# A routed two-layer graph network: pair loads that wait for their own chunk's sends, and an allotment issued in pieces

## The chip, the cores and the metric

The kernel runs on one core of a Trainium2 chip. The core has a tensor engine (PE, with its weight loads shown apart as PEld), a vector engine (DVE), a scalar engine (ACT), GpSimd (POOL), and SyncE (SP), which here only issues transfers; 16 DMA engines move data between HBM and the on-chip memory for all of them. Each engine works off its own list of instructions in order and waits on semaphores for the others. The metric is the device time of one execution in microseconds (us), the median of several runs.

## The reference

The input `x` is 64 batches of 256 rows of 256 numbers (float32); `adj` is one 256 x 256 adjacency shared by all batches. Two layers run one after the other:

```
x = x + gnn0(layernorm(x))        # 4 heads, softmax over neighbours, elu
x = x + layernorm(x) @ Wf.T + bf
x = x + gnn1(layernorm(x))        # 1 head, relu
x = x + moe(layernorm(x))         # 8 experts, the two best of each row

def moe(tokens):
    probs = softmax(tokens @ router_w.T)
    rw, re = top_k(probs, 2);  rw = rw / rw.sum(-1)
    out = tokens
    for e in range(8):
        y = gelu(tokens @ w1[e] + b1[e]) @ w2[e] + b2[e]
        out = out + combine[:, e] * y      # combine: rw at re, else 0
```

The last step matters here: each row is sent to two of eight experts.

## The kernel before

**Work and tiles.** Each batch is two tiles of 128 rows. `batch_layers` computes the first three lines of the reference and the normalised rows `xng` for one batch; PE does the transposes and products, DVE and ACT the attention and the norms, and POOL the inverse roots (`rstd`, lines 407, 408, 445, 448). Near the end (`at_end`) DVE computes these roots itself.

**Routing.** Of the 64 batches 61 are routed, in 20 chunks: twelve of four batches, then five of two and three of one. The last three batches are dense: every expert is computed for every row and weighted. For a chunk, `route` finds the two best experts of each row (`top_two`), counts rows of each expert with two small products (`pp`), and gets each row's place in a region of its expert in a buffer `xs` in HBM. `send` (line 1054) then writes 128 rows of 260 numbers with one indirect DMA issued by POOL (line 1056), two for each tile: 244 sends in all. A step of the program sends one tile, so a chunk of four batches is sent over eight steps.

**Pairs.** Every 256 rows of one expert make a pair, and a full pair can be computed. `allot` (line 826) works out which pairs a chunk completed. It is 19 small DVE instructions in a generator of four parts: lines 833 to 839, 842 to 851, 854 to 862, 864 to 870. It gives `ids` (the expert and the place of each pair), which SP reads into registers (lines 881, 885), and `ef`. For a chunk of four batches (`spread`) the parts are issued at four of its tiles; for a smaller chunk all four are issued at once by `in_one`, ahead of the sends.

`expert_pair` computes one pair: SP loads its rows from `xs` (`xr`, four DMAs, line 892, and `xt`, line 903) and the expert's first weights (`we`, line 917); DVE turns the rows (`sT`); PE makes `ph` (line 950), ACT the Gelu (`hT`, line 956), PE `py` (line 965), DVE adds the bias (`y`, line 975), ACT scales the rows (line 943). Then `scatter` adds the 256 rows to the output with two indirect DMAs of POOL (line 986). Each scatter waits for the two adds before it (line 983), and for the plain stores (`out_dram<-base`, line 735) that precede it. There are 129 pairs: 115 full ones and 14 of the flush, which holds what is left in each expert's region. Before the flush is loaded, SP writes `fill` behind the last row of each of the eight regions (line 1168), at places that it reads from `ends_at` (line 1162).

**Waits.** A framework derives waits from what instructions read and write. `xs` is one tensor addressed through registers, so it takes any two accesses for a conflict unless told otherwise. Sends and fills are told not to wait for each other or for loads (group "rows"). A pair load is not told so: it waits for every send and fill issued before it in the program, besides those in `needs`, its own chunk's.

**Order.** The program is written under a manual schedule. All work consists of generators with a rank; in each step the active ones are advanced by rank, lowest first, and `yield r` gives the rank in the next step (a negative number: later in the same step). A batch begins every three steps. Until step 177 (`DRAIN_AT`) up to two pairs begin in every three steps, afterwards one in each step, and one scatter is issued per step for each pair that is ready. The order of the instructions on each engine is fixed by this when the kernel is built. Buffers: `xr` 5, `we` 7, `sT` 3, `hT` 5, `y` 9, `xt` 14.

Of the kernel before, what the change touches and what calls it, by code (L numbers as in the profile page):

```python
# [17 lines left out]
SYNC = mybir.DependencyQuery.ANY_SYNC  # L18
AFTER = mybir.DependencyInfo(mybir.DependencyClass.Sync, mybir.DependencyReason.DATA)
# [8 lines left out]
def kernel(  # L28
# [23 lines left out]
    NT = N // P  # L52
# [23 lines left out]
    keep = ctx.enter_context(tc.tile_pool(name="keep", bufs=1))  # L76
# [416 lines left out]
    for i in range(2):  # L493
        t = keep.tile([P, NT, D + 1], F32, tag=f"q1_{i}", name=f"q1_{i}")
# [280 lines left out]
    def in_one(parts):  # L775

        got = None
        for got in parts:
            pass
        return got  # L780
# [38 lines left out]
    rows = [keep.tile([P, E], F32, tag="rows", name="rows")]  # L819
# [56 lines left out]
    def expert_pair(j, n, ids, ef, regs, needs):  # L876

        i = j % GROUP
        upto = min(j + GROUP, n)
        if i == 0:  # L880
            _, regs["e"] = nc.values_load_multi_w_load_instructions(
                ids[0:1, 0, j:upto], engines=[mybir.EngineType.SP], min_val=0, max_val=E - 1,
                skip_runtime_bounds_check_because=WHY,
            )
            _, regs["t"] = nc.values_load_multi_w_load_instructions(
                ids[0:1, 1, j:upto], engines=[mybir.EngineType.SP], min_val=0, max_val=E * CAP,
                skip_runtime_bounds_check_because=WHY,
            )
        e_sp, t_sp = regs["e"][i], regs["t"][i]
        xr = io.tile([P, PAIR // S, KT * S], F32, tag="xr", name="xr", bufs=XBUFS)  # L890
        loads = [
            nc.sync.dma_start(  # L892
                out=xr[g * S : (g + 1) * S],
                in_=xs_d.rearrange("(t c q) f -> t q c f", c=PAIR // S, q=S)[
                    bass.ds(t_sp, 1), :, :, g * KT * S : (g + 1) * KT * S
                ].rearrange("t q c f -> (t q) c f"),
            )
            for g in range(P // S)
        ]

        xt = small.tile([P, 2, ROW - D], F32, tag="xt", name="xt", bufs=14)
        loads.append(
            nc.sync.dma_start(
                out=xt,
                in_=xs_d.rearrange("(t k p) c -> t p k c", p=P, k=2)[
                    bass.ds(t_sp, 1), :, :, D:
                ].rearrange("t p k c -> (t p) k c"),
            )
        )
        for load in loads:  # L910
            tc.add_to_no_dep_group("rows", load.ins)
            for name in needs:
                tc.add_manual_dep(
                    load.ins, name, AFTER, reason="any sent row may lie in the pair"
                )
        we = io.tile([P, WROW], F32, tag="we", name="we", bufs=WBUFS)
        nc.sync.dma_start(
            out=we, in_=wpack[bass.ds(e_sp, 1), :, :].rearrange("e p c -> (e p) c")
        )
        yield 90  # L920

        yield 95 if more else 75
        xT = turned(work.tile([P, KT, PAIR], F32, tag="sT", name="sT", bufs=3), xr)
        w = small.tile([P, 2], F32, tag="w", name="w", bufs=12)
        yield 30
        yield 30
        hT = hidden(xT, we)
        yield -65
        nc.vector.scalar_tensor_tensor(
            w[:, :, None], xt[:, :, 1:2], ef[:, j : j + 1], xt[:, :, 2:3],  # L930
            op0=ALU.is_equal, op1=ALU.mult,
        )
        nc.vector.tensor_tensor(w[:, :, None], w[:, :, None], xt[:, :, 3:4], ALU.add)
        yield 80
        if i == 0:
            _, regs["x"] = nc.values_load_multi_w_load_instructions(
                ids[0:1, 0, j:upto], engines=[mybir.EngineType.PE, mybir.EngineType.DVE],
                min_val=0, max_val=E - 1, skip_runtime_bounds_check_because=WHY,
            )
        y = result(hT, bass.ds(regs["x"][i], 1))  # L940
        yield 2
        for t in range(2):
            nc.scalar.activation(y[:, t, :], y[:, t, :], AF.Copy, scale=w[:, t : t + 1])  # L943
        scatters.append((y, xt))
# [103 lines left out]
    sent = []  # L1048
# [5 lines left out]
    def send(xe, at):  # L1054

        d = nc.gpsimd.indirect_dma_start(  # L1056
            out=xs_d[: E * CAP * PAIR, :],
            out_offset=bass.IndirectOffsetOnAxis(ap=at, axis=0), in_=xe, in_offset=None,
        )
        tc.declare_no_dep(  # L1060
            d.ins, query=SYNC, group="rows", reason="sent rows are all different, and none is in a full pair"
        )
        tc.add_to_no_dep_group("rows", d.ins)
        sent.append(d.ins.name)
        nc.gpsimd.nop()

    def later(rank, *phases):
# [5 lines left out]
    def route(c, row0, nt, n, last, xng, lg):  # L1073
# [3 lines left out]
        spread = nt == NTC  # L1077
# [5 lines left out]
        parts = top_two(c, nt, lg, tail[:, :, 0])  # L1083
# [50 lines left out]
        for i, xe in enumerate(xng):  # L1134
            vec.tensor_copy(xe[:, :, D + 1 :], tail[:, i * NT : (i + 1) * NT, :])
        parts = allot(c, n, False)
        if n and not spread:
            ids, ef = in_one(parts)
        if last:
            ends_at = rt([E], "ends_at", 2, I32)  # L1140
            vec.tensor_copy(ends_at, rows[0])
# [2 lines left out]
        for t in range(nt):  # L1144
            for k in range(2):
                send(xng[t // NT][:, t % NT, :], pos[:, k, t : t + 1])
            if n and spread and t in (1, 2, 4, 5):
                ids, ef = next(parts) or (None, None)
            if not last:
                yield 95  # L1150
            elif t % 2:
                yield 95
        needs = sent[mark:]
        if n:
            regs = {}
# [2 lines left out]
            )  # L1158
        if last:
            parts = allot(c + 1, FLUSH, True)  # L1160
            ids2, ef2 = in_one(parts)
            _, ends_sp = nc.values_load_multi_w_load_instructions(
                ends_at[0:1, :], engines=[mybir.EngineType.SP], min_val=0,
                max_val=(E * CAP - 1) * PAIR, skip_runtime_bounds_check_because="rows of a region",
            )
            filled = []
            for e in range(E):
                d = nc.sync.dma_start(  # L1168
                    out=xs_d[bass.ds(ends_sp[e], PAIR), :].rearrange("(p t) c -> p t c", t=2),
                    in_=fill,  # L1170
                )
                tc.declare_no_dep(
                    d.ins, query=SYNC, group="rows", reason="filling rows lie behind an expert's last row"
                )
                tc.add_to_no_dep_group("rows", d.ins)
                filled.append(d.ins.name)
                nc.sync.nop()
            yield 95
            regs2 = {}
            waiting.extend(  # L1180
                lambda j=j: expert_pair(j, FLUSH, ids2, ef2, regs2, filled)
                for j in range(FLUSH)
            )
# [131 lines left out]
```

## Time and profile before

| what | value |
|---|---|
| median of 3 runs | 1519.05 us (1517.03 to 1519.11) |
| the profiled execution | 1516.68 us |
| its span, first to last instruction | 1514.9 us |
| mean granted clock of PE over the span | 0.985 |
| sends (line 1056): number, mean on POOL | 244, 1089 ns |
| scatters (line 986): number, mean on POOL | 258, 1604 ns |
| HBM read and written | 146.00 MB, 88.35 MB |
| SP's longest waits | L622 for DVE 176.7 us, L735 for ACT 123.9 us, L892 for sends 121.1 us |

Times in a timeline count from the span's start. The durations in the profile are of one execution, so sums are made against its own 1516.68 us. A row such as `SPq L892 <- DMA xs<-xng,pos` reads: the queue of SP stood at line 892 until a DMA that writes `xs` from `xng` had landed. Busy time of POOL in a scatter or send is the time of writing its descriptors; the transfer runs on behind it. Where a releaser is named that can't be needed (an `hT` for a scatter), it merely ended at about the same time.

### The profile page before, as it was taken

What the parts mean: (1) busy time and instruction counts of PE and PEld (TensorE: products, weight loads), DVE (VectorE), ACT (ScalarE), POOL (GpSimd) and SP (SyncE); (2) the same over time, 40 slices, a digit from 0 to 9 for tenths busy, and PEclk for the clock granted to TensorE, in tenths of its full rate; (3) what the DMA queues carried; (4) which work ended last, traced back from release to release, by engine and by line L of the source; (5) the groups of instructions that cost most, each with busy time, mean ns of one, the idle gap of its engine ahead of it and who ended that gap; (6) DMA issues with size and microseconds to landing.
All of it is one profiled execution on the core that took longest, in us unless ns stands there. A gap on an engine that the chain in (4) does not pass through costs nothing. (4 is left out here: it accounts for less than half of the span.)

```text
span 1514.9 us, 29999 instructions
## 1 busy us (share of the span) xinstructions
PE 1421.4 (94%) x8134; PEld 1261.2 (83%) x8134; DVE 1245.9 (82%) x4419; ACT 1017.4 (67%) x2396; POOL 875.8 (58%) x845
## 2 busy tenths in 40 slices
PE   7899999999999999999999999998899989699992
PEld 6698888789898989999998989997788877578881
DVE  7689999989898889888898989899888878654541
ACT  1477667677778777777777777776678779553330
POOL 2122546455858586767676676756747776544444
PEclk9999999999999999999999999999999999999996
DMA  4822334576878788787877787867768676797743
GB/s 129 244 91 73 117 103 139 134 178 158 198 154 192 162 194 171 170 183 166 181 181 164 175 185 160 187 156 166 172 154 186 132 162 128 174 208 156 142 65 52
DMA packets 354355, 236.38 MB, mean 156 GB/s; under 512 B 246276, under 2 KB 316428, under 8 KB 354188
## 3 DMA queue, kind: packets, MB, share of 16 engines
q1 hardware_dynamic: 301272, 158.16, 41.7%
q0 software_dynamic: 48864, 66.33, 24.3%
q10 hardware_dynamic: 4052, 9.98, 2.1%
q8 instruction: 67, 1.10, 0.3%
q14 instruction: 100, 0.82, 0.2%
HBM read 146.00 MB, written 88.35 MB: 155 GB/s over the span
## 5 line engine op out<-in xcount | busy, mean ns | idle before, releaser
L986 POOL DMA_INDIRECT out_dram<-y,xt x258 | 413.9, 1604 | 195.7 <-issue 66.6
L585 PE MATMUL pv<-q,z 128*128 128x65 f32 (+1 forms) x2560 | 362.6, 296 | 0.4
L585 PEld LDWEIGHTS pv<-q,z 128*128 128x128 f32 x2560 | 329.9, 193 | 13.0 <-DVE z L571 1.1
L1056 POOL DMA_INDIRECT xs<-xng,pos x244 | 265.7, 1089 | 65.4 <-issue 59.8
L965 PE MATMUL py<-w2s,hT 128*128 (+1 forms) x1224 | 280.6, 380 | 6.3 <-ACT hT L956 6.3
L965 PEld LDWEIGHTS py<-w2s,hT 128*128 128x128 f32 x1224 | 228.3, 190 | 38.3 <-ACT hT L956 9.1
L950 PE MATMUL ph<-sT,we 128*128 128x256 f32 x1032 | 244.2, 387 | 14.9 <-DMA we<-wpack 8.8
L571 DVE SCALAR_TENSOR_TENSOR z<-z,q,mask 128x256 f32<-128x256 f32 x504 | 231.5, 482 | 14.7 <-DMA z<-terms 5.7
L950 PEld LDWEIGHTS ph<-sT,we 128*128 128x128 f32 x1032 | 198.0, 194 | 43.6 <-issue 10.3
L460 ACT COPY xT<-pt 128x512 f32<-128x512 f32 x209 | 121.3, 588 | 99.2 <-PE pt L454 76.6
L943 ACT ACTIVATE y<-y,w 128x256 f32<-128x256 f32 x258 | 112.9, 498 | 110.2 <-DVE y L975 93.6
L956 ACT ACTIVATE hT<-ph,we 128x256 f32<-128x256 f32 x306 | 123.9, 473 | 63.0 <-PE ph L950 42.4
L407 POOL TENSOR_SCALAR rstd<-mv 128x4 f32<-128x4 f32 (+1 forms) x66 | 15.6, 236 | 248.1 <-DVE mv L380 194.7
L425 ACT ACTIVATE off<-x,sums 128x256 f32<-128x256 f32 x256 | 129.4, 505 | 7.9 <-DVE x L668 1.7
L505 PE MATMUL pq<-wx,xT 128*128 128x259 f32 x512 | 125.3, 387 | 9.6 <-ACT xT L460 6.9
L470 PE MATMUL pq<-wx,xT 128*128 128x268 f32 x512 | 128.1, 394 | 1.5 <-ACT xT L460 0.7
L975 DVE TENSOR_TENSOR y<-py,b2s 128x512 f32<-128x512 f32 x129 | 85.9, 685 | 52.4 <-PE py L965 39.4
L661 PE MATMUL pf<-wfT,xT 128*128 128x256 f32 x512 | 122.7, 383 | 0.0
L505 PEld LDWEIGHTS pq<-wx,xT 128*128 128x128 f32 x512 | 94.3, 189 | 30.2 <-ACT xT L460 13.5
L470 PEld LDWEIGHTS pq<-wx,xT 128*128 128x128 f32 x512 | 97.8, 192 | 20.7 <-DVE wx L168 1.3
L689 ACT ACTIVATE rel<-pv,rinv 128x256 f32<-128x256 f32 x128 | 54.4, 470 | 84.5 <-DVE rinv L592 53.8
L661 PEld LDWEIGHTS pf<-wfT,xT 128*128 128x128 f32 x512 | 93.8, 193 | 10.4 <-issue 0.2
(174 smaller groups left out, 2383.7 us busy)
## 6 DMA issues: line engine op xcount, KB each, us to landing
we<-wpack SPq DMA_DIRECT2D x145, 288.0 KB
xr<-xs SPq DMA_DIRECT2D x516, 64.0 KB
z<-terms SPq DMA_DIRECT2D x46, 512.0 KB
xin<-in_x_dram SPq DMA_DIRECT2D x64, 256.0 KB
out_dram<-base SPq DMA_DIRECT2D x61, 256.0 KB
xblk<-in_x_dram SPq DMA_DIRECT2D x188, 64.0 KB
z<-terms ACTq DMA_DIRECT2D x17, 512.0 KB
out_dram<-y,xt POOLq DMA_INDIRECT x258
```

Of the source, the lines that this page charges most:

```text
L425: nc.scalar.activation(off, src[:, t, :], AF.Square, bias=sums[:, t : t + 1], scale=-float(D), accum_out=sq[:, at + t : at + t + 1],)
L460: nc.scalar.copy(dst, pt)
L470: nc.tensor.matmul(pq.rearrange("p h c -> p (h c)"), xT[:, k, t * P : (t + 1) * P], wx[:, k, :], start=(k == 0), stop=(k == KT - 1),)
L505: nc.tensor.matmul(pq, xT[:, k, t * P : (t + 1) * P], wx1[:, k, :], start=(k == 0), stop=(k == KT - 1),)
L571: nc.vector.scalar_tensor_tensor(z[:, j, :, h, :], terms, q[:, j, h, HD + 2 : HD + 3], masks[0][:, j, :].rearrange("p (t i) -> p t i", t=N ...
L585: nc.tensor.matmul(pv[:, h, :], z(j, h, t), q[:, j, h, : d + 1], start=(j == 0), stop=(j == NT - 1),)
L661: nc.tensor.matmul(pf[:, t, :], xT[:, k, t * P : (t + 1) * P], wfT[:, k, :], start=(k == 0), stop=(k == KT - 1),)
L950: nc.tensor.matmul(ph[:, f, :], we[:, k * D + f * P : k * D + (f + 1) * P], xT[:, k, :], start=(k == 0), stop=(k == KT - 1),)
L956: nc.scalar.activation(hT[:, f, :], ph[:, f, :], AF.Gelu, bias=we[:, C_B1 + f : C_B1 + f + 1])
L965: nc.tensor.matmul(py[:, t, :], hT[:, f, t * P : (t + 1) * P], w2s[:, e, f * D : (f + 1) * D].rearrange("p e c -> p (e c)"), start=(f == 0 ...
L986: d = nc.gpsimd.indirect_dma_start(out=out_rows, out_offset=bass.IndirectOffsetOnAxis(ap=xt[:, t, 0:1].bitcast(I32), axis=0), in_=y[:, t, ...
L1056: d = nc.gpsimd.indirect_dma_start(out=xs_d[: E * CAP * PAIR, :], out_offset=bass.IndirectOffsetOnAxis(ap=at, axis=0), in_=xe, in_offset=None,
```

## The change

Three things are edited.

- In `expert_pair`, the five loads of rows are declared independent of all instructions in a new group "sent", which holds every send and every fill, except those in `needs`: the sends of the pair's own chunk, or, for the pairs of the flush, the eight fills. `sent` and `filled` now hold instructions in place of names.
- In `route`, `allot` of a chunk of two batches (four tiles) is issued part by part behind the sends of its tiles 0, 1, 2 and 3; of a chunk of one batch (two tiles) two parts behind tile 0 and two behind tile 1. Chunks of four batches keep theirs at tiles 1, 2, 4 and 5. The chunk that is last now takes a step for each tile like the others, so its four sends are issued in two steps.
- The flush allotment is issued a part at a time ahead of every second fill, and the eight fills over two steps, four in each.

The order in which the instructions stand on the engines follows from the build. PE and ACT keep theirs exactly. On DVE the 19 instructions of each small allotment move from one block ahead of `by` and `stats` (lines 706, 379) to four places, each behind a `y` addition or behind a part of the next routing. On POOL the last chunk's four sends in a row become two, then the two adds of a scatter and an iota, then two. On SP the block of eight fills ahead of the pair loads becomes one pair load, four fills, one pair load, four fills.

```diff
--- before.py
+++ after.py
@@ -908,10 +908,14 @@
             )
         )
         for load in loads:
+            tc.declare_no_dep(
+                load.ins, query=SYNC, group="sent", keep=needs,
+                reason="the pair's rows were sent by these or by sends that earlier loads waited for",
+            )
             tc.add_to_no_dep_group("rows", load.ins)
-            for name in needs:
+            for ins in needs:
                 tc.add_manual_dep(
-                    load.ins, name, AFTER, reason="any sent row may lie in the pair"
+                    load.ins, ins.name, AFTER, reason="any row of these may lie in the pair"
                 )
         we = io.tile([P, WROW], F32, tag="we", name="we", bufs=WBUFS)
         nc.sync.dma_start(
@@ -1061,7 +1065,8 @@
             d.ins, query=SYNC, group="rows", reason="sent rows are all different, and none is in a full pair"
         )
         tc.add_to_no_dep_group("rows", d.ins)
-        sent.append(d.ins.name)
+        tc.add_to_no_dep_group("sent", d.ins)
+        sent.append(d.ins)
         nc.gpsimd.nop()
 
     def later(rank, *phases):
@@ -1134,8 +1139,7 @@
         for i, xe in enumerate(xng):
             vec.tensor_copy(xe[:, :, D + 1 :], tail[:, i * NT : (i + 1) * NT, :])
         parts = allot(c, n, False)
-        if n and not spread:
-            ids, ef = in_one(parts)
+        turns = (1, 2, 4, 5) if spread else (0, 1, 2, 3) if nt == 2 * NT else (0, 0, 1, 1)
         if last:
             ends_at = rt([E], "ends_at", 2, I32)
             vec.tensor_copy(ends_at, rows[0])
@@ -1144,12 +1148,9 @@
         for t in range(nt):
             for k in range(2):
                 send(xng[t // NT][:, t % NT, :], pos[:, k, t : t + 1])
-            if n and spread and t in (1, 2, 4, 5):
+            for _ in range(turns.count(t) if n else 0):
                 ids, ef = next(parts) or (None, None)
-            if not last:
-                yield 95
-            elif t % 2:
-                yield 95
+            yield 95
         needs = sent[mark:]
         if n:
             regs = {}
@@ -1158,13 +1159,14 @@
             )
         if last:
             parts = allot(c + 1, FLUSH, True)
-            ids2, ef2 = in_one(parts)
             _, ends_sp = nc.values_load_multi_w_load_instructions(
                 ends_at[0:1, :], engines=[mybir.EngineType.SP], min_val=0,
                 max_val=(E * CAP - 1) * PAIR, skip_runtime_bounds_check_because="rows of a region",
             )
             filled = []
             for e in range(E):
+                if e % 2 == 0:
+                    ids2, ef2 = next(parts) or (None, None)
                 d = nc.sync.dma_start(
                     out=xs_d[bass.ds(ends_sp[e], PAIR), :].rearrange("(p t) c -> p t c", t=2),
                     in_=fill,
@@ -1173,9 +1175,11 @@
                     d.ins, query=SYNC, group="rows", reason="filling rows lie behind an expert's last row"
                 )
                 tc.add_to_no_dep_group("rows", d.ins)
-                filled.append(d.ins.name)
+                tc.add_to_no_dep_group("sent", d.ins)
+                filled.append(d.ins)
                 nc.sync.nop()
-            yield 95
+                if e % 4 == 3:
+                    yield 95
             regs2 = {}
             waiting.extend(
                 lambda j=j: expert_pair(j, FLUSH, ids2, ef2, regs2, filled)
```

## The prediction

> **What bounds the kernel now.** I read the page first, then windows by stage, the waits of each engine, and last the timelines. The page's engine row says TensorE:
>
> ```profile
> PE 1421.4 (94%) x8134; PEld 1261.2 (83%) x8134; DVE 1245.9 (82%) x4419; ACT 1017.4 (67%) x2396; POOL 875.8 (58%) x845
> ```
>
> The windows split that average (columns: stretch, its us, then PE, PEld, DVE, ACT and POOL busy with counts, PE clock, DMA share, GB/s):
>
> ```profile
> 350.00:1000.00 650.00, 649.57 (x3861) 586.54 (x3860) 583.34 (x2000) 495.90 (x1173) 448.11 (x420) 1.00 0.80 176
> 1000.00:1260.00 260.00, 240.76 (x1348) 211.30 (x1347) 223.04 (x882) 190.84 (x418) 172.49 (x160) 0.98 0.71 158
> 1260.00:1440.00 180.00, 161.39 (x750) 138.41 (x750) 109.75 (x409) 94.75 (x206) 85.95 (x63) 0.98 0.79 165
> 1440.00:1515.00 75.00, 46.97 (x214) 39.99 (x213) 23.38 (x52) 16.00 (x38) 33.95 (x22) 0.85 0.40 58
> ```
>
> Up to 1000 us PE is idle 0.4 us in 650: nothing beside it counts there. From 1000 to 1260 (the chunks of two batches and of one) it is idle 19.2 us. After 1260 another thing rules. The chain of waits shows PE from 1337 to 1470 and the scatters on POOL after it, but the waits of POOL between 1260 and 1515 tell another story: it stands before L986 in nearly every pair, with releasers that change at random.
>
> ```profile
> POOL out_dram L986 <- DMA out_dram<-y,xt: 43.2, 12, 5.2
> POOL out_dram L986 <- ACT hT L956: 29.3, 11, 3.8
> POOL out_dram L986 <- DMA xr<-xs: 23.1, 5, 5.8
> ```
>
> An `hT` or an `xr` releases no scatter; each scatter waits, by L983, for the two adds before it. So I compared two timelines: the scaled `y` of a pair on ACT (L943) and its scatter on POOL, 129 of each in one order. The y of the pair scattered at 1260.43 was ready at 1243.6, that of 1336.75 at 1310.0, of 1434.78 at 1401.5: 17, 27 and 33 us earlier. From 1260 on the scatters are one serial chain that never waits for data: 34 intervals from 1260.43 to 1504.88, 7.19 us each. At the end, with little else on the DMAs, they show their bare form on POOL's timeline:
>
> ```profile
> 1498.58 1.54 POOL L986 DMA_INDIRECT out_dram<-y,xt  x1 [2.95 <-DMA out_dram<-y,xt]
> 1500.43 1.54 POOL L986 DMA_INDIRECT out_dram<-y,xt  x1 [0.30 <-issue]
> 1504.88 1.54 POOL L986 DMA_INDIRECT out_dram<-y,xt  x1 [2.91 <-DMA out_dram<-y,xt]
> ```
>
> So the end is: when POOL can begin this chain, plus 34 intervals. It begins behind the last `rstd` that POOL must wait for, L445 at 1253.13 (idle 4.11, released by ACT `off`), and ACT came to that behind the y of a PE product that ended at 1246.8. Before 1250, therefore, PE's time still counts one for one. Its gaps there, from PE's timeline (start, us, ..., idle before and releaser):
>
> ```profile
> 1043.24 3.72 PE L950 MATMUL ph<-sT,we 128*128 128x256 f32 x16 [2.92 <-DVE sT L117]
> 1051.89 1.36 PE L505 MATMUL pq<-wx,xT 128*128 128x259 f32 x5 [1.91 <-ACT hT L956]
> ...
> 1092.33 1.07 PE L454 MATMUL pt<-ident,x 128*128 128x128 f32 x4 [4.47 <-DVE x L695]
> ```
>
> Others are 1.03 at 1133.30, 1.04 at 1183.05, 1.78 at 1218.35 and 1.67 at 1234.27. Before most of them DVE runs unbroken, with the allotment in front:
>
> ```profile
> 1080.15 0.17 DVE L833 TENSOR_SCALAR full<-run 128x8 f32<-128x8 f32 x1
> ...
> 1083.51 0.17 DVE L870 TENSOR_SCALAR ids<-pair_of 128x4 int32<-128x4 f32 x1
> ...
> 1088.19 1.29 DVE L117 STREAM_TRANSPOSE sT<-xr 128x512 f32<-128x512 f32 x2
> ...
> 1092.19 0.47 DVE L668 SCALAR_TENSOR_TENSOR x<-pf,rstd,x1b 128x256 f32<-128x256 f32 x1
> ```
>
> The 19 small instructions take 3.53 us, and all behind them, `x` of L668 too, comes 3.53 us later.
>
> **What the Trainium skill says.** "TensorE: Matmul & The Clock Gate", the part on array architecture, calls the queues of ACT and DVE strict FIFO: what stands behind the allotment cannot pass it. The trace agrees (no instruction between 1080.15 and 1092.6 starts out of its order). Its Part 1 says that an idle window of about 3.4 us halves PE's clock. The trace agrees: clock 0.50 in 1092.80 to 1096.20, behind the gap of 4.47, and in 1236.20 to 1239.50. "DMA: Bandwidth & Descriptors", Anatomy of one DMA, puts most of a DMA's fixed 2 us into the confirmation of its last byte, and says a semaphore wait is held by the issuing sequencer. Here the wait for a scatter's landing is what spaces the chain, and a pair load that waits on SP holds all of SP's queue.
>
> **The change part by part.** The built order of the changed kernel against the old shows PE and ACT with the same instructions in the same order. DVE, SP and POOL move.
>
> 1. Pair loads no longer wait for later chunks' sends. SP loses most of one row:
>
> ```profile
> SPq L892 <- DMA xs<-xng,pos: 121.1, 24, 9.2
> ```
>
> In chunks of four batches three of the first loads in each group drop one such wait (4 to 6 us each). Behind it on SP stood a `we` load, `terms`, `xin` and `base`. Their users are covered: PE is full until 1000; later `sT` stands 1 to 10 us ahead of its product, and after 1260 the scatters have 17 us in hand. DVE waits for `z<-terms` only 5.7 us in the whole run. Bounds: a gain of 2, a loss of 2 (loads that are earlier meet other transfers); I take 0.
>
> 2. The flush pairs' fills leave the way of ordinary loads. Before, eight fills (5.93 us on SP from 1311.63, the last landing taking 4.57) stood before the load at 1321.58, and PE waited 8.75 us for the pair at 1328.40. In the new order one pair load precedes the fills, another comes between the fours, and no ordinary load waits for a fill. The PE gap mostly goes, but the scatters were 23 us or more behind then: worth 0. Were that cover absent it would be worth 8.75 and 3.4 of a halved clock (6.83 us at half), 12 in all: the upper bound.
>
> 3. Allotment in pieces: 4, 7, 4 and 4 instructions, 0.8, 1.1, 0.8 and 0.9 us from the same rows, one at the end of each of the next steps, chunks of one batch two and two. DVE's sum is the same. Piece one now stands behind `y` (L975), before the `sT` of the next step. Gap by gap: at 1043.24 the lump took 3.78, 0.8 comes back, 2.98 earlier: the 2.92 goes. The 1.91 at 1051.89 hangs on the same late `ph` (one batch earlier it is 0.74): 1.15 goes. At 1092.33, 3.53 less 0.8: 2.7 goes. At 1133.30 and 1183.05 `sT` stood directly behind the lump: 1.0 each. At 1234.27 the lump of 1220.77 to 1224.25 is at the head of an unbroken row: 1.6. The 1.78 at 1218.35 waits for POOL's `rstd`, with no lump before it: stays. Sum 10.35. In return the pieces stand before `x`/`z`, `by` and `sT`, in five chunks: between 0 and 5 x 1.1 = 5.5, I take 2.5, since most `sT` have over 1.1 us in hand but two have 1.55. Net gain 7.9. POOL can follow: its idle waits for `rstd` there (9.97 at 1136.55, 3.85 at 1186.30, 4.11 at 1253.13) stand right behind lumps or PE work and shrink with them. If both halved clocks go as well, 3.4 us x half each, 3.4 more: kept for the range.
>
> 4. The last chunk sends two and two. Its four sends in a row (1300.57 to 1305.46) sit inside the serial chain, in an interval of 8.93 us where the neighbours have about 7.1. Two sends fit behind the adds' landing. The two that move, 2.6 us with their issue, fall into the next interval, which is idle 3.29. Between 1.8 gained and 1 lost; I take a gain of 1.2.
>
> 5. The flush allotment (3.83 us on DVE at 1301.60) split by the fills: behind the scatters' backlog, 0.
>
> Sum: -7.9 - 1.2 = -9.1. Against the profiled execution (span 1514.9, execution 1516.68) this is 1507.6. The median shown, 1519.05, is 2.4 above that; moved by the same 9.1 it gives 1510.
>
> **The rivals.**
> A, the forecast, 1510 (own range 1504 to 1515.5): chance 0.52.
> B, the gaps only move. DVE is busy 223 of 260 us from 1000 to 1260, and the same work stays in the queue; PE could meet `z` or `by` late instead. Only the split sends and a little remain, about 1.5: 1517.5. For it: DVE's density. Against: DVE does wait for PE in between (1.9 us at `lg`, 1.2 at `rinv` from 1050 to 1100), so it has room to catch up. 0.20.
> C, slower: denser DMA stretches the scatters. At a DMA share of 0.40 an interval is 6.35; from 1336.75 to 1434.78, at about 0.79, 7.54: 3 us per unit of share. If loads freed of waits raise the share by 0.1 through 26 intervals, that is 8; with B's 1.5 gained it ends at +6: 1525. It decides once the mean of 34 intervals rises above 7.19 + 9.1/34 = 7.46. Against: bytes are the same, so what crowds early leaves late. 0.15.
> D, the larger gain: halved clocks vanish (3.4) and the loads end sooner against the scatters, whose intervals fall towards 6.35 earlier (five intervals by 1): 1510 - 8.4, about 1502. 0.13.
>
> **How the numbers follow.** About 0.2%, 3 us, is what a measurement of this kernel can tell from no change. Faster (below 1516): A 0.50, D 0.13, B 0.04: 0.67. Within: B 0.15, A 0.02: 0.17. Slower: C and a rest of B: 0.16. The range 1502 to 1521 leaves out most of C and half of D.
>
> **What would show it.** Right: gaps before `ph` at 1043 and `pt` at 1092 under 2 us, the first of the last 35 scatters some 8 us earlier, its distance to the end 1 to 2 us shorter, SP's L892 row for sends a fraction of 121, no 8.75 gap near 1328, and no time saved by that. Wrong: new PE gaps behind `z`, `by` or `sT`; intervals of the last scatters above 7.46; or scatters found waiting for their `y`, so that PE rules to the end.

## The result, and the profile after

| | before | after |
|---|---|---|
| median | 1518.04 us (4 runs, 1516.12 to 1519.11) | 1508.78 us (4 runs, 1505.69 to 1511.43) |
| ratio, with its 95% interval | | 0.9943 (0.9917 to 0.9969) |
| the profiled execution | 1516.68 us | 1511.43 us |
| its span | 1514.9 us | 1509.6 us |
| 34 intervals between the scatters of the last 35 pairs | 244.4 us | 239.3 us |

The change makes the kernel 9.3 us faster by the medians; the profiled execution of the changed kernel is its slowest of four, so that the two traces differ by 5.3 us only. All lines from 912 on stand four or five numbers later (`ph` L950 is L954, the scatter L986 is L990, the send L1056 is L1060, `y` L975 is L979).

The windows of the changed kernel (same columns as before: stretch, its us, then PE, PEld, DVE, ACT and POOL busy, PE clock, DMA share, GB/s):

```profile
350.00:1000.00 650.00, 645.44 (x3817) 581.20 (x3816) 578.77 (x1983) 493.74 (x1163) 444.27 (x417) 1.00 0.76 174
1000.00:1260.00 260.00, 248.53 (x1421) 219.03 (x1419) 231.59 (x906) 199.60 (x445) 174.52 (x165) 0.99 0.74 167
```

From 1000 to 1260 PE is idle 11.5 us in place of 19.2. But from 350 to 1000, where it had been idle 0.4, it is now idle 4.6. The waits of SP's queue, longest first, have lost the row that waited for sends (121.1 us). No row of that kind is left; SP now stands longer further down its list, at L622 (176.7 us before):

```profile
SPq L622 <- DVE stats L379: 327.7, 44, 11.4
SPq L735 <- ACT base L724: 136.6, 15, 11.3
```

PE's timeline at the two largest of the old gaps (2.92 at 1043, 4.47 at 1092):

```profile
1052.55 1.32 PE L954 MATMUL ph<-sT,we 128*128 128x256 f32 x5 [0.79 <-PE pf L661]
...
1099.89 0.84 PE L454 MATMUL pt<-ident,x 128*128 128x128 f32 x4 [0.78 <-issue]
```

And POOL's at the end, where each pair still waits about 3 us for the landing of the adds before it:

```profile
1493.25 1.55 POOL L990 DMA_INDIRECT out_dram<-y,xt  x1 [3.02 <-DMA out_dram<-y,xt]
1495.11 1.55 POOL L990 DMA_INDIRECT out_dram<-y,xt  x1 [0.30 <-issue]
1499.62 1.55 POOL L990 DMA_INDIRECT out_dram<-y,xt  x1 [2.96 <-DMA out_dram<-y,xt]
```

**Where the time went.** PE carries out the same instructions in the same order in both kernels, so its instructions can serve as milestones. I take those that began at 350, 1000 and 1245 us in the trace of before, and for the rest the start of the last 35 scatters and of the last pair's scatter:

| stretch | before | after | difference |
|---|---|---|---|
| start to milestone 350 | 350.1 | 356.5 | +6.4 |
| 350 to 1000 | 650.0 | 655.8 | +5.8 |
| 1000 to 1245 | 245.0 | 233.3 | -11.7 |
| 1245 to the start of the scatter chain | 15.3 | 14.7 | -0.6 |
| the chain, 34 intervals | 244.4 | 239.3 | -5.1 |

The gain is where the prediction put it. Two stretches that the prediction took for unchanged took as much back, before any small chunk was allotted. A milestone difference between two single traces can be the change's or the execution's; the experiments were made to tell which.

### The profile page after: what moved, and what is told of

It reads as the page before. It is cut to its first block, busy times and chain, and to the rows that moved or that the text cites. A ratio compares the mean times of both kernels' runs of the same rounds, so it can differ in the third digit from the quotient of the medians.

```text
span 1509.6 us, 29981 instructions
## 1 busy us (share of the span) xinstructions
PE 1426.9 (95%) x8134; PEld 1264.8 (84%) x8134; DVE 1245.8 (83%) x4419; ACT 1017.4 (67%) x2396; POOL 871.6 (58%) x845
## 5 line engine op out<-in xcount | busy, mean ns | idle before, releaser
L990 POOL DMA_INDIRECT out_dram<-y,xt x258 | 413.1, 1601 | 194.7 <-issue 57.2
L585 PE MATMUL pv<-q,z 128*128 128x65 f32 (+1 forms) x2560 | 366.6, 298 | 0.6
L585 PEld LDWEIGHTS pv<-q,z 128*128 128x128 f32 x2560 | 333.0, 194 | 13.6 <-DVE z L571 1.7
L1060 POOL DMA_INDIRECT xs<-xng,pos x244 | 260.7, 1068 | 65.3 <-issue 59.0
L571 DVE SCALAR_TENSOR_TENSOR z<-z,q,mask 128x256 f32<-128x256 f32 x504 | 231.5, 482 | 17.6 <-DMA z<-terms 8.6
L954 PE MATMUL ph<-sT,we 128*128 128x256 f32 x1032 | 240.0, 382 | 2.5 <-DVE y L979 1.0
L954 PEld LDWEIGHTS ph<-sT,we 128*128 128x128 f32 x1032 | 195.6, 192 | 30.2 <-DVE y L979 1.4
L460 ACT COPY xT<-pt 128x512 f32<-128x512 f32 x209 | 121.6, 590 | 110.7 <-PE pt L454 79.5
L505 PE MATMUL pq<-wx,xT 128*128 128x259 f32 x512 | 128.8, 394 | 15.1 <-ACT xT L460 10.0
L979 DVE TENSOR_TENSOR y<-py,b2s 128x512 f32<-128x512 f32 x129 | 85.4, 684 | 53.9 <-PE py L969 41.8
L505 PEld LDWEIGHTS pq<-wx,xT 128*128 128x128 f32 x512 | 95.6, 192 | 37.9 <-ACT xT L460 17.7
```

The costliest lines, as they stand in the source:

```text
L460: nc.scalar.copy(dst, pt)
L505: nc.tensor.matmul(pq, xT[:, k, t * P : (t + 1) * P], wx1[:, k, :], start=(k == 0), stop=(k == KT - 1),)
L571: nc.vector.scalar_tensor_tensor(z[:, j, :, h, :], terms, q[:, j, h, HD + 2 : HD + 3], masks[0][:, j, :].rearrange("p (t i) -> p t i", t=N ...
L585: nc.tensor.matmul(pv[:, h, :], z(j, h, t), q[:, j, h, : d + 1], start=(j == 0), stop=(j == NT - 1),)
L954: nc.tensor.matmul(ph[:, f, :], we[:, k * D + f * P : k * D + (f + 1) * P], xT[:, k, :], start=(k == 0), stop=(k == KT - 1),)
L990: d = nc.gpsimd.indirect_dma_start(out=out_rows, out_offset=bass.IndirectOffsetOnAxis(ap=xt[:, t, 0:1].bitcast(I32), axis=0), in_=y[:, t, ...
```

## The experiments

They ran in four groups. The kernels of one group ran on one chip, beside the kernel before, and each ratio compares within its group. An edit to the kernel before or to the changed kernel is shown as a short diff, cut to the lines that matter. The traces of e5 and e9 are of the slowest execution of their kernel (1506.23 and 1512.56 us) and that of e6 is 4 us above its median; so stretches of traces are compared below, and whole kernels by their times.

| kernel | median, us | kernel before beside it | ratio (95% interval) |
|---|---|---|---|
| e1 loads alone | 1507.86 | 1511.85 | 0.9975 (0.9958 to 0.9992) |
| e2 pieces alone | 1500.43 | 1511.85 | 0.9923 (0.9893 to 0.9952) |
| e3 sends alone | 1508.69 | 1511.85 | 0.9969 (0.9955 to 0.9983) |
| e4 flush alone | 1511.07 | 1511.85 | 0.9996 (0.9979 to 1.0014) |
| e5 the changed kernel again | 1500.99 | 1514.98 | 0.9890 (0.9863 to 0.9917) |
| e6 changed, no pieces | 1512.75 | 1514.98 | 0.9980 (0.9963 to 0.9996) |
| e7 changed, more PE work | 1503.37 | 1514.98 | 0.9920 (0.9892 to 0.9947) |
| e8 changed, roots on DVE earlier | 1498.36 | 1514.98 | 0.9881 (0.9841 to 0.9920) |
| e9 changed, no loads | 1503.18 | 1517.11 | 0.9912 (0.9880 to 0.9944) |
| e10 changed, no split sends | 1512.52 | 1517.11 | 0.9970 (0.9951 to 0.9990) |
| e11 e8 and an earlier drain | 1505.17 | 1517.11 | 0.9932 (0.9913 to 0.9950) |
| e12 loads alone again | 1512.51 | 1514.19 | 0.9987 (0.9973 to 1.0000) |

### One part at a time (e1 to e4)

**e1**, the loads alone (and the list of sends and fills kept as instructions, in the group "sent"):

```diff
         for load in loads:
+            tc.declare_no_dep(load.ins, query=SYNC, group="sent", keep=needs, ...)
             tc.add_to_no_dep_group("rows", load.ins)
```

> The kernel before with part 1 alone: pair loads independent of all sends and fills but their own chunk's. Theory (the gain is the allotment's pieces and the split sends): within 3 us of the kernel before (1518), PE gaps of 2.9 at 1043 and 4.5 at 1092 still there. Rival 1 (the gain comes from the loads, which the row of 121 us on SP suggests): 5 to 9 us faster. Rival 2 (earlier loads crowd the transfers; PE gets gaps of about 0.65 before L505 between 350 and 1000 as in the changed kernel's trace, 4 us in all): up to 5 us slower, and those gaps are seen here too.

**e2**, the pieces alone:

```diff
-        if n and not spread:
-            ids, ef = in_one(parts)
+        turns = (1, 2, 4, 5) if spread else (0, 1, 2, 3) if nt == 2 * NT else (0, 0, 1, 1)
...
-            if n and spread and t in (1, 2, 4, 5):
+            for _ in range(turns.count(t) if n else 0):
                 ids, ef = next(parts) or (None, None)
```

> The kernel before with part 3 alone: the allotment of chunks of two batches and of one issued in pieces; the last chunk's four sends stay in one step, loads keep all their waits. Theory: 6 to 9 us faster than before (about 1510), PE idle 7 to 8 us less between 1000 and 1260, the first of the last 35 scatters 8 us earlier. Rival (gaps only move, or the pieces help only together with loads that are earlier): within 3 us. PE gaps of 0.65 before L505 between 350 and 1000: none, if they belong to the loads.

**e3**, the last chunk's sends over two steps:

```diff
-            if not last:
-                yield 95
-            elif t % 2:
-                yield 95
+            yield 95
```

> The kernel before with part 4 alone: the last chunk's four sends over two steps, which also puts the flush allotment and the fills a step later. Theory: 1 to 2 us faster, the interval of scatters that holds the sends 7.1 in place of 8.9 us; too little to tell from no change by the time alone. Rival (the whole flush a step later costs as much as the split gains, or the interval only moves to the next pair): 0, and the two intervals together stay at about 16.1 us.

**e4**, the flush allotment and the fills:

```diff
-            ids2, ef2 = in_one(parts)
...
             for e in range(E):
+                if e % 2 == 0:
+                    ids2, ef2 = next(parts) or (None, None)
...
-            yield 95
+                if e % 4 == 3:
+                    yield 95
```

> The kernel before with part 5 alone: the flush allotment a part ahead of every second fill, the fills over two steps. Theory: within 2 us of the kernel before, though PE's wait of 8.75 us at 1328 shrinks. Rival (PE's wait sets the end): 4 to 8 us faster.

**Measured.** The pieces carry most: 0.9923 in e2, which is 11.6 us of 1511.85 (single kernels' gains are worked out from the ratio so; the medians give the same to 0.3 us for the four parts but e3, where they give 3.2 in place of 4.7). From milestone 1000 to 1245 the trace of e2 takes 230.7 us, those of e1, e3 and e4 take 243.8, 242.9 and 242.3. Of e2's gaps in that stretch 10.3 us are left; e1, e3 and e4 have 14.6 to 16.8, before had 19.0. The first of the last 35 scatters is at 1247.3 in e2 and at 1257.4 to 1260.6 in the other three.

The loads alone gave 3.8 us (1.2 to 6.3 by the interval), where 2 were allowed for, and the sends alone 4.7 (2.6 to 6.8), more than the 1.2 forecast. The flush gave nothing. None of the four shows the PE gaps of 0.65 us before L505 between 350 and 1000: all take 648.0 us there with no gap at all. So rival 2 of e1 did not appear on this chip.

The traces also part what the prediction had put together in the gap of 8.75 us near 1328. PE's gap there in e4 and in e1, from their timelines:

```profile
1331.63 1.62 PE L950 MATMUL ph<-xT,we 128*128 128x256 f32 x3 [9.37 <-DMA we<-wpack]
```

```profile
1330.72 1.39 PE L969 MATMUL py<-w2s,hT 128*128 128x256 f32 x4 [2.50 <-ACT hT L960]
```

Fills over two steps alone leave PE waiting 9.4 us for weights `we`, so the fills' new place is not what closes the gap. Loads without waits leave 2.5. But they are not the only way: with the old waits kept, the pieces alone leave 3.2 (e2, at 1316.5), and pieces, sends and flush together 2.2 (e9, at 1329.4). What the gap costs is not told by e4, nor by e3 (9.36 at 1333.8), since the kernel before has it too. That it is covered rests on the scatters: behind it they come 22 us or more after their `y` in both.

### The whole again, and without the pieces (e5, e6)

e5 is the changed kernel itself. **e6**, the pieces taken out of it:

```diff
+        if n and not spread:
+            ids, ef = in_one(parts)
...
-            for _ in range(turns.count(t) if n else 0):
+            if n and spread and t in (1, 2, 4, 5):
                 ids, ef = next(parts) or (None, None)
```

> The changed kernel once more, beside the others of this group. The parts alone gave 0.9975 (loads), 0.9923 (pieces), 0.9969 (sends) and 0.9996 (flush) of the kernel before. Theory 1 (the parts add; the small PE gaps before L505 between 350 and 1000 in its first trace were that execution's own): 0.986 to 0.989, and a trace without those gaps. Theory 2 (the parts overlap, since the loads and the pieces compete for the same gaps behind 1245): 0.991 to 0.995, as first measured. If the small gaps return, they belong to the combination of the parts.

> The changed kernel with the allotment of small chunks in one block again (loads, sends and flush stay changed). Theory of the prediction (pieces carry nearly all): 0.998 to 1.000 of the kernel before, PE 11 to 13 us longer between landmarks 1000 and 1245 than in the changed kernel. Rival (loads and sends are worth 3 to 5 us each, as each alone seemed to be): 0.993 to 0.996.

**Measured.** On this chip the changed kernel is at 0.9890, 16.7 us (12.6 to 20.8) less than before, or 14.0 by the medians; theory 1. Its trace has no gap between 350 and 1000 and takes 648.0 us there. Without the pieces it is at 0.9980: the pieces carry 11.8 us (1512.75 less 1500.99; 13.6 by the ratios), and loads, sends and flush together 2 to 3 (0.6 to 5.6 by the interval). That is less than the 8.5 that e1 and e3 gave one by one. It points to two parts that do not add, but the lower ends of their intervals sum to 3.8, so the times alone do not show it.

Over all kernels with the same roots, 1000 to 1245 takes 242.3 to 245.0 us in the six traces with the block and 230.7 to 238.2 in the six with the pieces.

What is late next shows in e5 behind 1245. The last chunk but one has a single batch, and its second two parts of the allotment (here eight instructions of L854 to L870, from 1257.04 on) fall right ahead of the roots that DVE computes by itself at the end (L404 to L398) and of the `x` that PE waits for. From the timelines of DVE and PE:

```profile
1257.04 0.16 DVE L854 TENSOR_TENSOR past<-ends,jrow 128x16 f32<-128x16 f32 x1
...
1258.46 0.17 DVE L870 TENSOR_SCALAR ids<-pair_of 128x2 int32<-128x2 f32 x1
1258.54 0.16 DVE L404 TENSOR_SCALAR var<-mv 128x2 f32<-128x2 f32 x1
...
1260.50 0.16 DVE L398 SCALAR_TENSOR_TENSOR rstd<-root,rstd 128x2 f32<-128x2 f32 x1
...
1262.40 0.48 DVE L668 SCALAR_TENSOR_TENSOR x<-pf,rstd,x1b 128x256 f32<-128x256 f32 x1
...
1262.94 1.12 PE L454 MATMUL pt<-ident,x 128*128 128x128 f32 x4 [4.00 <-DVE x L668]
```

In the block's kernels this gap is 1.5 us; here it is 4.0, in the first trace of the changed kernel 6.0. With a stretch at half clock that begins near it in both traces (10.2 and 6.8 us; before has none there), it costs PE 5 to 6 us between milestones 1262 and 1280 (18.0 before, 23.3 and 24.1 after). No scatter of the chain waited for that: in both traces each comes 11 us or more behind its `y`.

### Is it the chain? (e7, e8)

**e7** makes half of the second product twice for ten of the 14 pairs of the flush, the same values again in the same place:

```diff
-        for t in range(2):
+        for t in (0, 0, 1) if again else range(2):
```

**e8** moves the inverse roots to DVE one batch earlier:

```diff
-        return order_steps[-1] >= TICKS * (B + 2)
+        return order_steps[-1] >= TICKS * (B + 1)
```

> The changed kernel with half of the second product done twice for ten of the 14 pairs of the flush: 4 more products of 0.38 us each, 15 us of PE in all, late. Theory (after 1260 the serial scatters rule and PE has over 20 us in hand): within 3 us of the changed kernel in the same group, the lag of the last scatters behind their y down from 22 to about 7 us. Rival (PE sets the end): 15 us slower.

> The changed kernel with the inverse roots of the last batches moved from POOL to DVE three steps (one batch) earlier, so that POOL no longer waits for the last one before the chain of scatters. Theory (the chain begins behind that wait): interval 93 falls from about 12 to 7 or 8 us, the whole ends 3 to 5 us earlier than the changed kernel. Rival (DVE, with 11 more small instructions per root pair in its densest stretch, delays PE by as much): no change or up to 4 us slower.

**Measured, e7.** Between the `y` of pair 110 and of pair 128 PE's line takes 128.8 us in place of 120.2: the added products cost 8.6, not 15 (their records of 0.38 us each overlap). The kernel is 2.4 us slower by the medians, within the bound of 3, and 4.5 by the ratios, whose intervals overlap; the times alone would not settle it. The lag does: the last scatter stands 19.2 us behind its `y` in place of 24.1, and none of the chain less than 10. So an end set by PE is not what is seen; the chain's 34 intervals took 245.0 in place of 241.4, which accounts for the rest of the lag, and whether that comes from the added work is not shown.

**Measured, e8.** POOL's timeline at the start of the chain, e5 first, then e8:

```profile
1243.17 1.61 POOL L990 DMA_INDIRECT out_dram<-y,xt  x1 [0.30 <-issue]
1246.34 0.19 POOL L445 TENSOR_SCALAR rstd<-sq 128x4 f32<-128x4 f32 x1 [1.56 <-ACT off L425]
...
1253.06 1.62 POOL L990 DMA_INDIRECT out_dram<-y,xt  x1 [0.30 <-issue]
```

```profile
1231.03 1.61 POOL L990 DMA_INDIRECT out_dram<-y,xt  x1 [1.09 <-ACT hT L960]
1232.95 1.56 POOL L990 DMA_INDIRECT out_dram<-y,xt  x1 [0.30 <-issue]
...
1240.04 1.62 POOL L990 DMA_INDIRECT out_dram<-y,xt  x1 [0.30 <-issue]
```

With the root gone, interval 93 (from the last scatter before the chain to its first) is 9.0 us in place of 11.8, and the chain begins 11.5 us after milestone 1245 in place of 14.7. In all other kernels with POOL's root, before and after, it begins 14.5 to 15.4 after it. So the chain does hang on PE's progress through that root, as the prediction read it. But its 34 intervals then took 245.8 in place of 241.4, and the kernel is at 0.9881 against 0.9890 (2.6 us by the medians, where 3 to 5 were expected, with intervals that overlap): what was gained at the start isn't shown at the end.

### Loads against sends (e9, e10, e12), and an attempt at more (e11)

**e9** is the changed kernel without e1's edit, **e10** the changed kernel without e3's, **e12** is e1 again. **e11** is e8 with

```diff
-    DRAIN_AT = TICKS * (B - 5)
+    DRAIN_AT = TICKS * (B - 6)
```

> The changed kernel with the loads' old waits (pieces, sends and flush stay). Alone the loads were worth 0.9975. In the two traces of the changed kernel the two intervals that hold the split sends sum to 17.5 us, with the sends alone split to 13.2. Theory 1 (loads without waits crowd the transfers there, and take back what the split gives): the two intervals sum to 13 to 15 us here, and the whole is no slower than the changed kernel, 0.986 to 0.990. Theory 2 (the loads gain by themselves, as they did alone): 0.991 to 0.994.

> The changed kernel with the last chunk's four sends in one step again (loads, pieces and flush stay). Theory 1 (with the loads free the split is worth nothing): the same as the changed kernel, 0.987 to 0.991, the two intervals at 16 to 18 us. Theory 2 (it keeps the 3 us it gave alone): 0.991 to 0.993, the two intervals 2 to 3 us longer than 17.5.

> The kernel before with part 1 alone, once more, for the stretch from landmark 350 to 1000, in which PE has all its work at hand. So far it took 648.0 us in eight traces, with the loads free in five of them, 650.0 and 650.2 in two with the old waits, and 655.6 to 656.0 in three with the loads free, where copies of xT on ACT (L460) and rinv on DVE (L592) wait up to the end of a scatter on POOL. Theory (the freed loads are free of cost where these waits don't occur, and cost some 5.5 us where they do): either 648.0 and 0.996 to 0.999 of the kernel before, or 655 to 656 and 0.999 to 1.003. Rival (the waits belong to the other parts of the change, which the three slow traces had too): where L460 waits for scatters at all, 650 and 0.996 to 0.998.

> The changed kernel with the inverse roots on DVE a batch earlier (0.9881 by itself) and the stage in which one pair begins in each step begun a batch earlier as well, for a version that beats both. Theory (the end is the start of the scatter chain plus its pairs, so pairs that are computed earlier shorten it until PE's own end rules, 11 us ahead of the last scatter): 3 to 8 us faster than 0.9881 of before. Rival (PE is full until 1000 and the pairs displace batches that the dense experts and the last chunk wait for): as much later.

**Measured at the sends.** The two intervals that hold the last chunk's sends (the scatters of pairs 99 and 100 to the next) sum to 13.2 and 13.7 us with sends split and loads waiting (e3, e9), to 15.2 to 17.6 with sends split and loads free (the first trace after, e5 to e8, e11), and to 15.8 to 17.2 with four sends in a row (before, e1, e2, e4, e10, e12). POOL's timeline shows why. In e3:

```profile
1302.32 0.98 POOL L1056 DMA_INDIRECT xs<-xng,pos  x1 [0.30 <-issue]
1303.84 1.61 POOL L986 DMA_INDIRECT out_dram<-y,xt  x1 [0.55 <-ACT y L943]
...
1308.99 0.98 POOL L1056 DMA_INDIRECT xs<-xng,pos  x1 [0.30 <-issue]
1310.47 1.61 POOL L986 DMA_INDIRECT out_dram<-y,xt  x1 [0.50 <-ACT y L943]
```

and in e5, the changed kernel:

```profile
1294.33 0.98 POOL L1060 DMA_INDIRECT xs<-xng,pos  x1 [0.30 <-issue]
1297.55 1.61 POOL L990 DMA_INDIRECT out_dram<-y,xt  x1 [2.24 <-DMA out_dram<-y,xt]
...
1302.70 0.98 POOL L1060 DMA_INDIRECT xs<-xng,pos  x1 [0.30 <-issue]
1306.93 1.61 POOL L990 DMA_INDIRECT out_dram<-y,xt  x1 [3.25 <-DMA out_dram<-y,xt]
```

After two sends POOL waits 0.5 us for the adds before in e3, and 2.2 and 3.3 us in e5. The free loads have moved into this stretch: over the two intervals the DMA share is 0.93 to 0.98 with loads free and sends split (first trace, e5 to e8; 0.78 in e11) and 0.57 to 0.66 with loads waiting (before, e2, e3, e4, e9). So the freed loads take back what the split sends give, at this place.

The intervals of e9 are those of its theory 1, its time is that of theory 2: it (0.9912) is no slower than the first measurement of the changed kernel (0.9943), and slower than e5 on another chip (0.9890), not separable from either. e10 came out at 0.9970, beyond what either theory expected, and 9.3 us slower than e9 by the medians. Their traces can't say where these 9.3 stand, since the two executions traced differ by 0.2 us only (e9's is its slowest). e10's two intervals (16.2) are no longer than the changed kernel's. What the split is worth in the whole is 4.7 us by e3's time, and as e10's interval overlaps that of the first measurement (0.9943), it may be nothing beside free loads.

**Measured from 350 to 1000.** The traces come in two kinds. I counted ACT's copies of `xT` (L460) that had been idle over 0.3 us and began more than 0.5 us behind the end of PE's `pt`, which they copy:

| loads | such copies, of all that were idle | 350 to 1000, us | traces |
|---|---|---|---|
| waiting | none of 33 | 648.0 | e2, e3, e4 |
| free | none of 32 or 33 | 648.0 | e1, e5, e6, e7, e8, e12 |
| waiting | 18 of 33, 18 of 32 | 650.0, 650.2 | before, e9 |
| free | 23, 23 and 24 of 32 | 655.6 to 656.0 | first after, e10, e11 |

In the nine traces of the first two rows every copy that had been idle begins within 0.04 us of the end of `pt`. Of the late ones in the other five traces, 9 to 16 in each begin within 0.1 us of the end of an indirect DMA that POOL was issuing, and so do 3 to 14 of DVE's reciprocals (L592), which read another product of PE.

In this stretch e9 and e10, of one group, differ in nothing but the loads. Where such waits occur, the freed loads cost some 5.5 us in this stretch; where they don't, nothing. The extra time stands before one product, `pq` of L505 (7.6 to 8.0 us over e1's trace in the three, 2.0 and 2.2 in before and e9). The timeline of the first trace of the changed kernel, all engines:

```profile
480.87 0.67 PE L454 MATMUL pt<-ident,xng 128*128 128x128 f32 x4
481.51 1.62 POOL L990 DMA_INDIRECT out_dram<-y,xt  x1 [0.31 <-issue]
483.09 0.18 DVE L592 RECIPROCAL rinv<-pv 128x4 f32<-128x4 f32 x1 [0.84 <-remote]
483.15 0.59 ACT L460 COPY xT<-pt 128x512 f32<-128x512 f32 x1 [2.94 <-remote]
...
490.38 1.80 PE L505 MATMUL pq<-wx,xT 128*128 128x259 f32 x7 [0.64 <-ACT hT L960]
```

and the same place in e5:

```profile
481.03 0.67 PE L454 MATMUL pt<-ident,xng 128*128 128x128 f32 x4
481.34 1.61 POOL L990 DMA_INDIRECT out_dram<-y,xt  x1 [0.30 <-issue]
481.74 0.58 ACT L460 COPY xT<-pt 128x512 f32<-128x512 f32 x1 [1.69 <-PE pt L454]
481.92 0.24 DVE L592 RECIPROCAL rinv<-pv 128x4 f32<-128x4 f32 x2
```

PE's `pt` ends at 481.54 in the first and at 481.70 in the second. In e5 ACT copies it at once, while POOL is writing the scatter's descriptors. In the first trace DVE and ACT start at 483.09 and 483.15, where POOL's scatter ends (481.51 + 1.62 = 483.13). From 483.95 on ACT then works without a break, so that its next copy of `xT` starts at 489.73 (488.69 in e5), and PE's `pq`, which reads it, is late by 0.64.

The view calls the releaser of these two waits "remote". The trace's record of semaphores names it: it is PE's own signal for `pt`. In e5 the signal is recorded at 481.71, 0.01 us behind the end of `pt`; in the first trace at 483.13, 1.59 behind it, and ACT starts 0.02 after the signal. All 106 late copies of the five traces start so, within 0.03 us of a signal of PE that comes 0.5 to 2.0 us late, and so do DVE's reciprocals. What ACT and DVE wait for is therefore a signal of PE that arrives late.

e12 was to separate the loads from the other parts in such an execution, and did not get one: 648.0 us, no such waits, 0.9987. That the cost belongs to the loads rests on e9 against e10 and e11, one trace each, with the first traces of before and after in the same pattern. (From 1000 to 1245 e9 and e10 differ the other way, 238.2 and 234.7.) The three are of one group, hence of one chip, and none of the nine traces of the other three groups of experiments shows such a wait; whether it goes with the chip or with the execution is open. It would fit that the whole change gained some 5 us less at the first measurement than in e5 (9.3 and 14.0 by the medians).

**e11** isn't better than the changed kernel by a margin that shows (0.9932 with those waits, against 0.9943 at the first measurement, which had them too). Interval 93 fell to 6.8 us and the chain began at 1248.9, but its intervals took 245.1. No version here is shown to beat the changed kernel.

### How far a chain tells parts apart

e1 and e12 are one kernel. Their 34 intervals took 234.2 and 244.0 us. Over all traces with the old tail of sends they took 234.2 to 244.4, with the split 239.3 to 246.3. So the 5.1 us by which the chain is shorter in the first trace of the changed kernel can't be put down to the change.

## Why the prediction was right, and where it was not

The forecast of 1510 was met (1508.78), and the side and the mechanism that it named as likeliest are the ones that the runs show. Point by point:

- **The bound.** Confirmed in two of three respects. The chain begins at a fixed 14.5 to 15.4 us after milestone 1245 in every kernel with POOL's last root, and earlier without it (e8). Once it runs it does not wait for PE: 8.6 us of added work left the last scatter 19.2 us behind its `y` (e7). Not shown is that a chain begun earlier for another reason than PE ends earlier: e8's began 3.2 us earlier and took 4.4 longer. That PE's time before it counts one for one rests on the pieces, whose gain of 10 to 14 us stands in the stretch from 1000 to 1245 and in the times alike (e2, e6).
- **Part 3, the pieces (-7.9).** The gaps fell from 19.0 to 11.3 us between 1000 and 1245, which is -7.7. The term left out of the sum and kept for the range, the halved clocks, came too: 10.2 us at half rate became 3.4, worth 3.4. The prediction counted two such stretches; the trace of before has a third, at 1219.1. It also read the one at 1236 as a case of the idle window of 3.4 us that it cites, which it is not: the gap before it is 1.67. With a remainder of 0.6 that is the -11.7 of the table (7.7 + 3.4 + 0.6), and e2 and e6 give 11.6 and 11.8 by the times. Of the single gaps, those at 1043 and 1092 fell to 0.79 and 0.78, 1.78 at 1218 stayed (1.81); the 1.91 at 1052 was to lose 1.15 and kept 1.88, and one of 0.61 at 1074 grew to 1.88 (at 1084), part of the 2.5 that was to be paid back. So the mechanism was right and the sum too small by the clocks.
- **Part 1, the loads (0, between -2 and +2).** Here a step failed: "PE is full until 1000" was taken as cover for whatever the loads displace. Alone they gave 3.8 and 2.0 us by the ratios (e1, e12), at or beyond the upper bound; where the copies of L460 come late they cost some 5.5 between 350 and 1000, in the stretch that was put at nothing. PE was full there, but with no margin to spare before `pq`.
- **Part 4, the split sends (-1.2).** Alone it did more, at the place named (16.1 to 13.2 us in e3). In the changed kernel the interval named fell to 8.0 but the next rose to 9.4, sum 17.5: the step assumed that "two sends fit behind the adds' landing", and the freed loads delay that landing. That is rival C's mechanism, at two intervals and not at 26. The mean of the 34 intervals was 7.04, far from the 7.46 from which C decides.
- **Part 2 and 5, fills and flush (0).** Nothing, as said (e4, 0.9996). The gap of 8.75 did not go with the fills' new place alone (9.37 in e4); it went with the freed loads (2.50 in e1), and as well with the pieces (3.22 in e2). The upper bound of 12 for it was too high in one term: of the 6.83 us at half clock there, from 1324.9 on, about half lie inside the gap, so that 1.7 and not 3.4 was at stake.
- **Rivals.** B is refuted by e2 and e6. A gain near D's 17.5 (16.7 us by the ratio, 14.0 by the medians, e5) was measured on a chip without the waits of L460; fewer halved clocks are in it, as D had it (3.4 us at half rate between 1000 and 1245 in e5's trace), shorter intervals of scatters are not shown.
- **The sum.** It was met in part by things that offset each other. Of the table, -11.7 is the change's. +5.8 is put down to the freed loads in an execution with those waits, by e9 against e10, one trace each. Of +6.4 up to 350, 1.2 arose before 285, some 3 is a halved clock of 10.2 us at 289, which follows a gap of 1.95 us there in nine of the 14 traces of before, after and the twelve runs and is absent in five, before among them; the other 2 is a gap of 1.65 us before L505 at 328, which e10 has too (1.68) and which looks like those of the next stretch. The chain's -5.1 is within what one kernel shows twice.

Left open: why PE's signals come late in some traces and not in others, and what the split sends are worth beside free loads.

## What to carry to other kernels

A block of small instructions on an in-order engine costs whatever waits directly behind it; cut it and put the parts where the next consumer has slack, and look at the one place where a part lands in front of another chain of small instructions. Where a wait is taken away from transfers, their users may be covered and the change still not free: they move, and what they then collide with (here the landing of adds that space a serial chain, and a tight product on a PE that is full) has to be looked for at their new place. Parts that gain one by one need not add: measure the whole without each.

## What the runs showed of the hardware that was not expected

- In five of 14 traces PE's signals come late, and only PE's: from 350 to 1000, 62 to 69 of its recorded semaphore signals stand over 0.06 us behind the end of any product that gives one, and none in the other nine; none of ACT's, DVE's or POOL's does in any trace. It goes with POOL's issue of indirect DMAs: of PE's signals due while POOL was writing descriptors 37 to 49% are recorded at once in the five, of the others 93 to 96%. In the nine it is at least 97% of both. In the same five traces 19 to 32% of the signals of PE, ACT and DVE have no record, so how many were late can't be counted, and whether the recording itself takes part is not shown. The Trainium skill ("SBUF — State Buffer", Terms) says that DVE and GpSimd share a port pair under an exclusive lock and that ACT has ports of its own. That is not what is seen here: ACT and DVE start as soon as PE's signal is there, and in the trace shown a DVE reciprocal started at 482.09, in the middle of the scatter. The cause is not settled.
- PE's clock was halved for 6.8 to 10.2 us near 289 after a gap of 1.95 us in nine traces, and stayed full after the same gap in five. At 1043 in the trace of before it stayed full after a gap of 2.92 us, and in the same trace gaps of 1.78 and 1.67 us (at 1218 and 1234) were followed by 3.4 us at half rate. The Trainium skill ("TensorE: Matmul & The Clock Gate", Part 1) gives an idle window of about 3.4 us; here a shorter gap did it in some executions and a longer one not in another, so for gaps of 1.7 to 3 us the price has to be kept as a range.
- Four more products per pair, with records of 0.38 us each, lengthened PE's line by 0.86 us per pair (8.6 for ten), not by 1.5.
